# Cross-attention and a quantised feed-forward block on one core: the first block of attention written anew, with work moved from VectorE to GpSimd and ScalarE

## The chip, the core and the metric

The kernel runs on one core of one Trainium2 chip. Its engines are TensorE (PE in the profile; PEld is its weight load), VectorE (DVE), ScalarE (ACT), GpSimd (POOL) and SyncE (SP, which here only starts transfers). Each works through its own queue of instructions in order, and they wait for one another by semaphores. Transfers are started on the queues of SP, POOL and ACT ("SPq", "POOLq", "ACTq" in the profile). The metric is the device time of one execution in microseconds, and the time of a kernel is the median of its runs. The profile comes from one execution, taken by the hardware profiler.

## What is computed

The reference, cut to what matters (`_proj(W, b, x)` is `einsum('oi,bil->bol', W, x) + b[:, None]`):

```python
# x, ctx: (32, 64, 512); 8 heads over the last axis, 64 wide
q = _proj(Wq, bq, layernorm(x)); k = _proj(Wk, bk, ctx); v = _proj(Wv, bv, ctx)
p = softmax(q_h k_h^T / 8)               # per head and batch, 64 x 64
x = x + _proj(Wo, bo, p v_h)
g = silu(layernorm(x) @ dequant(gate))   # 512 -> 1792
u = layernorm(x) @ dequant(up)
x = x + (g * u) @ dequant(down)          # 1792 -> 512
# dequant: (integer - zero) * scale, one zero and one scale
# per 128 input rows and column
```

The projections act on the 64 rows of a batch element, not on the 512 columns. All is float32.

## The kernel before

**Tiling.** Two batch elements of 64 rows fill the 128 partitions: a *pair*. There are 16 pairs, in 4 *blocks* of 4. For each block the kernel does the attention of its pairs, normalises the result, turns it over (`flip`, L557) into a high and a low part (`hTh`, `hTl`, 128x512 for each 128 input columns; `high` L580, `low` L583), and runs the feed-forward on the block: for each of 14 chunks of 128 hidden columns, `gate_up` (L633) does 4 steps of a gate product `pg` and an up product `pu` (four matmuls of 512 columns a step, L642), with a scaling by ScalarE after each of the first three steps (L652, by the quotient of neighbouring scales `s_q`), then SiLU (L655), the product with up (L658), its split into high and low (GpSimd, L668 and L669), and `down` (L674) with its products (L687, L690).

**Weights.** The integers stand in SBUF as float; their zeros are subtracted in place: gate (`ng`) and up (`nu`) by GpSimd (L309), a piece of 256 or 512 columns at a time, down (`nd`) by VectorE (L322). The zeros go to DRAM in 16 and 8 bits (`zeros`, cast by GpSimd, L153) and come back broadcast over the partitions (L289, L295). Weight columns are loaded in groups, the first of 256 columns, the second of 512, by transfers that GpSimd's queue starts (L273, L277).

**The head.** The attention of block 0 cannot lie beside a feed-forward. Its four pairs are done one by one, by a text, `START` (L778), that writes down the order in which steps are issued: "2.apply" is the step `apply` of pair 2. Within the head (`tc.manual_schedule()`, L800) every engine's queue has just this order. The steps of a pair:

- `stats` (VectorE, L396 to L398), `scale` (GpSimd, the power -1/2, L402), `apply` (VectorE, L112): layer norm of the pair's rows into `xn`.
- `k`, `q` (32 small products each, L421), `k_out`, `q_out` (VectorE, bias added on the way out of PSUM, L433); `v` (L456), `v_out` (ScalarE, L466).
- `scores` (L474), `highest` (L486), `less` (L489; both VectorE), `exp` (ScalarE, L502), `sums` (VectorE, L506 and L507), `divide` (GpSimd, L512).
- `turn` (L521; the weights of softmax times Wo), `turn_out` (ScalarE, L531), `weigh` (L538), `residual` (VectorE, two halves of 256 columns, adding the last bias and the rows, L551; then the store of the rows, L554, on SP).
- `stats2`, `scale2`, `apply2`, `flip`, `high`, `low`: the second layer norm and the turning over.

Steps without a pair: `projections` and `biases` lay out the small weights; `zeros`, `broadcast`, `more` (zeros); `gate`, `up`, `more_gate`, `more_up` (loads of weight columns, on GpSimd's queue); `rows` (load of the rows of pairs 4 and 5, on SP); `integers` (one piece L309 each); `scales` (L234, the scales transposed, and `scales_out`, L236); `quotients` (VectorE, L242 to L244, over 128x84); `warm` (idle products on PE, L571). Steps named "behind products" (L821) wait for the last PE work written before them. The head's PSUM tiles are four pairs of banks; they are given back before the first `pg`, so the first gate product (40.07 us in the profile) waits for the last `low`.

**Behind the head** the loop over rounds (L918) issues a step of each of two lanes of `gate_up`, of `down`, of block t+1's attention (`ROUND_STEPS`, L594; there two pairs are done together, "4to" in a tile's name is pairs 4 and 5), and weight pieces (at most so many a round, L910). There a scheduler sets each engine's order. The attention of later blocks has one PSUM tile of two banks (`ps_at`, L885) for all its products in turn: `pk`, `pv`, `pq`, `pss` and so on, each of which waits until the one before has been read. The rows `x` have three buffers (L126), so the rows of pairs 6 and 7 are loaded once those of pairs 0 and 1 have been stored and read for the last time.

## Time and profile before

| | |
|---|---|
| median of 3 runs | 438.89 us (438.71 to 439.97) |
| the profiled execution: its time, its span | 440.32 us, 438.2 us |
| granted TensorE clock, mean of the span | 0.99 |
| busy: PE, PEld, DVE, ACT, POOL | 408.2, 313.8, 329.7, 305.1, 281.7 us |
| last `hTl` of the head ends; first gate product starts | 39.82; 40.07 us |
| POOL's pieces of `nu`, first 256 columns | 30.87 to 34.54 us (start of the last 33.88) |
| POOL issues `ng`, `nu`, `nd` (second group) at | 30.02, 35.72, 36.53 us |
| ACT busy from 10 to 15 us | 0.00 us |
| DVE busy from 10 to 15 us | 4.86 us |

A row of the profile's groups or timeline names the line of the kernel, the engine, the operation, and "out<-in" by the tiles' names with partitions x columns; "x4" is how many instructions are merged in it. In brackets stands how long the engine had been idle and what ended that. The chain of waits follows the work that ended last back to the start, each piece to what released it; "issue" is time in which the engine waited for nothing that the profile shows. The table of stretches gives, for each stretch, each engine's busy time and number of instructions, the clock that TensorE was granted (1.00 is full), the share of the transfer engines and what they moved.

### The profile page before, as it was taken

Reading aid. Unit: us, or ns where it says so; the run is one execution under the profiler, and the core shown is the slowest. Engines: PE = TensorE matmul, PEld = TensorE weight load, DVE = VectorE, ACT = ScalarE, POOL = GpSimd, SP = SyncE. Lnnn points to the kernel's source line nnn. Section 1 sums busy time; section 2 is a strip of 40 time slices with the busy share of each in tenths; the row PEclk is TensorE's granted clock in tenths of the full one; section 3 lists DMA queues with packets and bytes.
Section 4 is the critical chain, followed back from the end, with each engine's and each line's share of the span. In section 5 each row is a group of like instructions: output and inputs, shape, how many; then the busy total and the mean of one; then the engine's idle time right before and its main releaser. Section 6 shows DMA issues by size and latency. Waiting matters only on the chain.

```text
span 438.2 us, 10356 instructions
## 1 busy us (share of the span) xinstructions
PE 408.2 (93%) x4191; PEld 313.8 (72%) x4191; DVE 329.7 (75%) x515; ACT 305.1 (70%) x468; POOL 281.7 (64%) x291
## 2 busy tenths in 40 slices
PE   3777989889999999999999999989999999999993
PEld 3655657557778786887778787767778888887772
DVE  4988476986879885895869885896869655768675
ACT  2243888347787769767888669776788778777771
POOL 4375849676844547575787668775787887774330
PEclk9999989989999999999999999999999999999998
DMA  6299739942021200321010103310000012110002
GB/s 213 60 270 362 246 125 287 331 146 74 1 74 48 72 29 0 96 100 49 1 50 0 52 1 97 96 49 1 1 14 38 1 49 88 57 49 0 2 4 99
DMA packets 20911, 36.54 MB, mean 83 GB/s; under 512 B 1832, under 2 KB 7416, under 8 KB 20856
## 3 DMA queue, kind: packets, MB, share of 16 engines
q1 hardware_dynamic: 14056, 24.20, 16.6%
q0 software_dynamic: 6192, 11.01, 8.7%
q8 instruction: 35, 0.57, 0.5%
q10 hardware_dynamic: 608, 0.59, 0.4%
q14 instruction: 20, 0.16, 0.1%
HBM read 27.37 MB, written 8.42 MB: 82 GB/s over the span
## 4 chain that ended last, share of the span: by engine, by line
PE 75%; DVE 12%; ACT 6%; POOL 3%; issue 2%; DMA 1%; SPq 0%; DVEq 0%; POOLq 0%; ACTq 0%
PE pu L642 21%; PE pg L642 21%; PE pd L687 11%; PE pd L690 10%; DVE y L700 3%; ACT pu L652 1%; ACT pg L652 1%; DVE xn_set L112 1%; DMA x<-in_x_dram 1%; DVE q_e_set L489 1%; PE py L715 1%; POOL ng L309 1%; ACT q_e_set L502 1%; ACT L502 1%; POOL q_e_set L512 1%
## 5 line engine op out<-in xcount | busy, mean ns | idle before, releaser
L700 DVE SCALAR_TENSOR_TENSOR y<-pd,s_all,y 128x512 f32<-128x512 f32 x204 | 150.1, 743 | 42.8 <-PE pd L690 39.7
L652 ACT ACTIVATE pg<-pg,s_q 128x512 f32<-128x512 f32 x168 | 111.7, 666 | 71.0 <-PE pg L642 69.7
L652 ACT ACTIVATE pu<-pu,s_q 128x512 f32<-128x512 f32 x168 | 111.1, 662 | 8.9 <-PE pu L642 7.9
L668 POOL CAST hh<-h 128x512 fp32r<-128x512 f32 x55 | 36.4, 663 | 96.7 <-DVE h L658 93.5
L687 PE MATMUL pd<-hh,nd 128*128 128x512 f32 x224 | 93.0, 415 | 2.8 <-DVE y L700 2.1
L642 PE MATMUL pg<-hTh,ng 128*128 128x512 f32 x224 | 90.9, 406 | 3.8 <-DVE hTl L585 1.6
L642 PE MATMUL pu<-hTh,nu 128*128 128x512 f32 x224 | 91.0, 406 | 1.2 <-POOL nu L309 0.8
L642 PE MATMUL pu<-hTl,nu 128*128 128x512 f32 x224 | 89.5, 399 | 0.0
L642 PE MATMUL pg<-hTl,ng 128*128 128x512 f32 x224 | 89.2, 398 | 0.0
L690 PE MATMUL pd<-hl,nd 128*128 128x512 f32 x224 | 89.1, 398 | 0.0
L669 POOL TENSOR_TENSOR hl<-h,hh 128x512 fp32r<-128x512 f32 x55 | 73.3, 1332 | 4.2
L658 DVE SCALAR_TENSOR_TENSOR h<-pu,s_all,g 128x512 f32<-128x512 f32 x56 | 41.8, 747 | 30.0 <-ACT g L655 20.0
L687 PEld LDWEIGHTS pd<-hh,nd 128*128 128x128 f32 x224 | 42.1, 188 | 19.8 <-DVE y L700 6.3
L339 POOL TENSOR_TENSOR squares<-squares 128x512 f32<-128x512 f32 (+1 forms) x46 | 55.1, 1199 | 1.6
L642 PEld LDWEIGHTS pg<-hTh,ng 128*128 128x128 f32 x224 | 42.4, 189 | 17.5 <-issue 2.7
L642 PEld LDWEIGHTS pu<-hTh,nu 128*128 128x128 f32 x224 | 42.5, 190 | 15.7 <-ACT pu L652 2.2
L642 PEld LDWEIGHTS pg<-hTl,ng 128*128 128x128 f32 x224 | 42.5, 190 | 9.5
L642 PEld LDWEIGHTS pu<-hTl,nu 128*128 128x128 f32 x224 | 42.7, 190 | 9.3
L655 ACT ACTIVATE g<-pg,s_all 128x512 f32<-128x512 f32 x56 | 38.9, 695 | 14.0 <-PE pg L642 12.4
L690 PEld LDWEIGHTS pd<-hl,nd 128*128 128x128 f32 x224 | 42.3, 189 | 8.1 <-DVE hl L666 0.2
L309 POOL TENSOR_TENSOR nu<-nu,z 128x512 fp32r<-128x512 f32 (+1 forms) x16 | 17.4, 1090 | 1.7 <-DMA nu<-in_L_ffn_up_w_dram 1.6
L309 POOL TENSOR_TENSOR ng<-ng,z 128x512 fp32r<-128x512 f32 (+1 forms) x16 | 17.1, 1077 | 0.0
(291 smaller groups left out, 464.8 us busy)
## 6 DMA issues: line engine op xcount, KB each, us to landing
c_set<-in_ctx_dram SPq DMA_DIRECT2D x6, 512.0 KB
x<-in_x_dram SPq DMA_DIRECT2D x6, 512.0 KB
z<-z_dram SPq DMA_DIRECT2D x6, 512.0 KB
ng<-in_L_ffn_gate_w_dram POOLq DMA_DIRECT2D x3, 1024.0 KB, 5.8
nu<-in_L_ffn_up_w_dram POOLq DMA_DIRECT2D x3, 1024.0 KB, 8.9
x_dram<-x SPq DMA_DIRECT2D x6, 512.0 KB
r<-x_dram SPq DMA_DIRECT2D x6, 512.0 KB
out_dram<-r SPq DMA_DIRECT2D x6, 512.0 KB
```

What stands on the lines that cost most here:

```text
L309: nc.gpsimd.tensor_tensor(piece, piece.bitcast(F32), z16[:, m, g, :], ALU.subtract)
L339: nc.gpsimd.tensor_tensor(total[:, :n], total[:, :n], square[:, :n], ALU.add)
L502: nc.scalar.activation(e, e, AF.Exp, scale=SCALE)
L642: nc.tensor.matmul(acc, w[:, g, ts(f, P)], half[:, g, :], start=(g == 0 and half is hi), stop=(g == KT - 1 and half is lo), skip_group_che ...
L652: nc.scalar.activation(acc, acc, AF.Copy, scale=by)
L655: nc.scalar.activation(g_sb, acc, AF.Silu, scale=by)
L658: ins = nc.vector.scalar_tensor_tensor(h_sb, acc, by, g_sb, ALU.mult, ALU.mult)
L668: nc.gpsimd.tensor_copy(hh, h_sb)
L669: ins = nc.gpsimd.tensor_tensor(hl, h_sb, hh.bitcast(F32), ALU.subtract)
L687: nc.tensor.matmul(pd, w, h_hi[t, f], start=(t, f) != LAST, stop=False, skip_group_check=True)
L690: nc.tensor.matmul(pd, w, h_lo[t, f], start=False, stop=True, skip_group_check=True)
L700: ins = nc.vector.scalar_tensor_tensor(y, pd, by, y, ALU.mult, ALU.add)
```

## The change

In block 0 only:

- Pairs 2 and 3: `apply` on GpSimd (`apply_pool`); k leaves PSUM by a ScalarE copy (`k_copy`) and gets its bias from GpSimd in SBUF (`k_bias`). Pairs 0 and 1 stay on VectorE.
- All four pairs: the last bias is added to the rows by ScalarE (`shift`), once `apply` and the statistics have read them; `residual` is then one tensor_tensor over 512 columns.
- `quotients` falls in three: `guards` (GpSimd: zero test and sum), the first two chunks' columns on VectorE at the end of the head (two reciprocals and two products of 128x6), and the other twelve chunks' columns in round 1 behind the head (two and two of 128x36). `s_inv` moves to a pool that lives on.
- `START` is written anew: pairs in the order 0, 2, 3, 1; the loads, integers, warm products and stores move with it.

```diff
-        def quotients():
-
-            s_inv = early.tile([P, 2, NS - FC], F32, tag="s_inv", name="s_inv")
+        s_inv = const.tile([P, 2, NS - FC], F32, tag="s_inv", name="s_inv")
+
+        def guards():
+
             later = s_all[:, 0:2, FC:]
-            nc.vector.scalar_tensor_tensor(s_inv, later, 0.0, later, ALU.is_equal, ALU.add)
-            nc.vector.reciprocal(s_inv, s_inv)
-            nc.vector.tensor_tensor(s_q, s_all[:, 0:2, : NS - FC], s_inv, ALU.mult)
+            nc.gpsimd.tensor_scalar(s_inv, later, 0.0, None, ALU.is_equal)
+            nc.gpsimd.tensor_tensor(s_inv, s_inv, later, ALU.add)
+
+        def quotients(fs: slice):
+
+            for m in range(2):
+                inv, num, quot = (
+                    a.rearrange("p (g f) -> p g f", f=FC)[:, :, fs]
+                    for a in (s_inv[:, m, :], s_all[:, m, : NS - FC], s_q[:, m, :])
+                )
+                nc.vector.reciprocal(inv, inv)
+                newest["DVE"] = nc.vector.tensor_tensor(quot, num, inv, ALU.mult).ins
...
+            def apply_pool(self):
+                nc.gpsimd.tensor_scalar(
+                    self.at["xn"][:, 0, :],
+                    self.x[:, 0, :],
+                    self.mv[:, 0, 0:1],
+                    self.rs,
+                    ALU.subtract,
+                    ALU.mult,
+                )
...
+            def k_copy(self):
+                nc.scalar.copy(self.by_bank("k_eT"), self.pk)
+
+            def k_bias(self):
+                k = self.by_bank("k_eT")
+                b = bqk[:, 1, :].unsqueeze(1).unsqueeze(1).to_broadcast([P, 2, self.n * KT, D])
+                nc.gpsimd.tensor_tensor(k, k, b, ALU.add)
...
             def residual(self):
                 x_heads = self.by_head(self.x)
+                if self.n == 1:
+                    x_h = x_heads.rearrange("p n h d -> p h n d")
+                    nc.vector.tensor_tensor(x_h, self.po, x_h, ALU.add)
+                    return self.keep_rows()
...
+            def shift(self):
+                nc.scalar.activation(self.x, self.x, AF.Identity, bias=bvo[:, 1:2])
...
         START = """
...
+            0.stats 0.scale 0.apply projections 1.stats biases projections_out
+            1.scale 2.stats 0.q biases_out 0.shift 3.stats 2.scale 2.k 2.apply_pool
+            0.k 2.k_copy 0.q_out 1.v 0.k_out 3.scale 2.shift 2.q 1.apply 3.apply_pool
+            1.v_out 0.scores 2.q_out 1.shift 3.k 0.highest 2.k_bias 3.shift 3.q
+            0.less 3.k_copy 1.q zeros 3.q_out 0.exp 2.scores 1.q_out 3.k_bias
+            broadcast 0.v 2.highest 1.k 0.v_out 2.less 2.v 1.k_out 2.exp 3.v 0.sums
+            2.v_out 1.scores gate 3.v_out 3.scores 1.highest 0.divide 3.highest
+            2.sums 0.turn 3.less 2.divide 0.turn_out 1.less 3.exp 0.weigh 2.turn
+            1.exp 3.sums up rows 2.turn_out 1.sums 3.divide 2.weigh 0.residual
+            1.divide 3.turn 2.residual 3.turn_out integers 2.stats2 1.turn more
+            integers scales 1.turn_out 0.stats2 3.weigh integers scales_out 1.weigh
+            integers 3.residual 3.warm 3.warm more_gate 3.stats2 0.scale2 1.residual
+            3.scale2 0.apply2 more_up 1.stats2 0.flip 1.warm 0.high 3.apply2 2.scale2
+            0.low 3.flip 1.scale2 2.apply2 3.high integers 1.apply2 2.flip integers
+            3.low 1.flip 2.high integers 1.high 2.low guards 1.low integers quotients
+            1.warm
...
                 elif step == "quotients":
-                    quotients()
+                    quotients(slice(0, FIRST // P))
+                elif step == "guards":
+                    guards()
...
+                if r == 1:
+                    with tc.issue_after(newest["DVE"]):
+                        quotients(slice(FIRST // P, FC))
```

Behind the head the order of the instructions on PE, ACT and POOL is unchanged. On DVE the second part of the quotients stands among the statistics of pairs 4 and 5, and the second `apply` of that set stands ahead of its `k_out` where it stood behind it.

## The prediction

> **What bounds the kernel now.** I read the page's busy shares first: PE 93% of the span, so after the head (everything before the first gate product) PE is the bound, and a change in the head can give at most what it brings that product forward, and only if block 1's first steps follow. So I read the chain of waits from 35 to 47 us (start, length, what):
>
> ```profile
> 37.06 0.69 DVE s_inv L243
> ...
> 37.77 0.24 DVE s_q L244
> 38.02 1.80 DVE hTl L585 x3
> 39.82 0.25 issue
> 40.07 0.70 PE pg L642 x2
> ...
> 44.48 0.64 PE pu L642 x2
> 45.11 1.02 PE pv_4to L456 x16
> ```
>
> The head ends on DVE: the last hTl at 39.82 lets PE start at 40.07, and the quotients stand ahead of three of the four hTl. From 40.07 the chain is PE, with pv of pairs 4 and 5 in it. Next, busy time by stretch (us; then PE, PEld, DVE, ACT, POOL, granted clock, DMA share, GB/s):
>
> ```profile
> 10.00:15.00 5.00, 4.97 (x212) 4.36 (x204) 4.86 (x13) 0.00 (x0) 1.67 (x4) 1.00 0.07 16
> 15.00:20.00 5.00, 3.13 (x140) 2.54 (x136) 4.90 (x10) 2.52 (x4) 1.06 (x2) 1.00 0.41 111
> 30.00:35.00 5.00, 2.90 (x13) 2.15 (x14) 4.70 (x12) 0.59 (x1) 4.54 (x9) 1.00 0.79 195
> ```
>
> DVE is full (4.7 to 4.9 of 5 us) while ACT and POOL have room until 20 us: the place the change draws from. Last, DVE's timeline after the head:
>
> ```profile
> 39.73 1.27 DVE L396 BATCH_NORM_STATS2 st_4to<-x 128x6 f32<-128x512 f32 x2
> 41.26 0.17 DVE L398 TENSOR_SCALAR rs_4to<-mv_4to 128x2 f32<-128x2 f32 x1
> 42.33 1.38 DVE L112 TENSOR_SCALAR xn_set<-x,mv_4to,rs_4to 128x512 f32<-128x512 f32 x1 [0.90 <-POOL rs_4to L402]
> 43.63 1.21 DVE L433 TENSOR_TENSOR k_eT_set<-pk_4to,bias 128x1024 f32<-128x1024 f32 x1
> 44.76 0.53 DVE L112 TENSOR_SCALAR xn_set<-x,mv_4to,rs_4to 128x512 f32<-128x512 f32 x1
> ```
>
> pv (L456) uses the PSUM tile that k's bias add (L433) reads, and there is one: pv starts at 45.04, 0.20 after that add ends (44.84). PE's weight loads waited 0.36 for it. So DVE's chain from hTl to L433 is already a second bound, just behind PE.
>
> **The head, part by part.** Taken off DVE: two normalisations (L112, 0.55 each: 1.1), two k biases (0.69 long, 0.62 apart: 1.25), the residual of four pairs from 0.82 (two halves) to about 0.62 (one tensor_tensor as L433: 4 x 0.2 = 0.8), and the quotients (0.24 + 0.68 + 0.24, about 1.1) from ahead of the last hTl. Together 4.2 us.
>
> Not all of it comes out. I set each engine's new written order out with these durations, each step starting at the later of its engine's free time and its last operand (0.05 us on, 0.16 from DVE to POOL). The same walk over the old order ends the last hTl at 40.2, against the 39.82 of the trace, so 0.35 is its error. Over the new order it gives 37.3, and 37.6 if DVE's normalisations lose time beside POOL. About 1.5 us turns into new DVE waits: 0.7 for pair 0's k, now third on PE in the stretch where 32 products took 1.1 us; 0.6 for pair 3's exp, behind pair 0's copy on ACT; the rest for pair 3's weigh and single latencies. Last hTl at **37.2, 2.6 earlier**; with an error of 0.7 either way.
>
> What I cost at nothing, and its cover. POOL's two normalisations are not in the trace: one input and two scalars, between the cast L668 (0.61) and the two-input L309 (1.17 with 512 columns). I take 0.85, and the walk's end doesn't move up to 1.8, since pair 2's q would wait only past 12.8 and xn is there at 10.9. POOL's k biases (1.04, as the division L512 x4): pair 2's is done at 13.7, read at 15.9; pair 3's at 16.6, read at 19.6. ACT's additions, four shifts (0.65, as the exp L502 or L466) and two k copies (0.57 as L531), 3.7 us, lie mostly in ACT's empty stretch; the last ends at 15.5, and pair 0's exp is wanted at 15.7, so past 0.2 us more each tenth delays that exp. POOL's queue: the zero casts go from 12.1 to 13.7, so the broadcast lands near 23, wanted at 27.4; the last nu piece ends at 37.8 instead of 34.5, read past 40; guards take some 0.6 between the pieces. The 512-column gate load stays at 30.0; up and down loads are issued at 31.9 and 32.7 instead of 35.7 and 36.5. On SP, the load of pairs 6 and 7 waits for the store of pair 1, now last; its rows are wanted near 62: 20 us of cover.
>
> Here a rule speaks against the change. The rows: two-input POOL work of 128x512 takes 1.04 to 1.17, the same size on DVE 0.69. The Trainium skill, "GPSIMD Engine Reference", opening and § 3.1, calls this engine the wrong choice for elementwise arithmetic, two inputs at half DVE's speed. By the rule alone the moved work loses; by the rows it has slack, and the sum stays.
>
> **Behind the head, where most of it is given back.** The new order of instructions on DVE has four small operations after the last hTl (first quotients), then the statistics of pairs 4 and 5 with two reciprocals of 36 columns among them, then *both* normalisations ahead of k's bias; before, one. A reciprocal took 0.20 for 8 columns (L507) and 0.68 for 84 (L243), so 0.38 for 36, some 0.34 apart, and 0.19 with a product of 0.18 for 6.
>
> 1. Last hTl 37.2; first quotients 2 x (0.19 + 0.18), 0.65 with overlap; statistics start 37.8.
> 2. To the end of rs_4to 1.70 (39.73 to 41.43) plus 0.68 for the reciprocals: 40.2.
> 3. POOL's power, 0.15 later and 0.72 long: 41.05. The two remaining products hide there.
> 4. Two normalisations. Alone 1.07 (2 x 0.535); beside POOL's subtractions:
>
> ```profile
> 86.53 2.27 DVE L112 TENSOR_SCALAR xn_set<-x,mv_4to,rs_4to 128x512 f32<-128x512 f32 x2
> ```
>
> Before, only the first (1.38) met one, since POOL then waited 1.65 for nu until 45.07. With nu loaded earlier, the second will meet one too. I take 2.05: 43.1.
> 5. k's bias 1.21: 44.3, pv at **44.5**, against 45.04.
>
> Behind pv every engine's order is as before, and PE (to 52) and ACT (to 60) carry the chain, so what is left at pv stays to the end. As a sum: 2.6 from the head, less 0.67 (the statistics started 0.09 ahead of the last hTl's end, now 0.6 behind), less 0.68 (reciprocals), less 0.75 (2.05 of normalisations where 1.30 stood, 42.33 to 43.63) = **0.5 us**. The profiled execution took 440.32 (span 438.2), the median of the runs is 438.89; I take the difference from each: 439.8 for such an execution, **438.4** for the median.
>
> Bounds: last hTl 0.7 each way; normalisations 1.07 to 2.98 (twice the slowest, 1.49 at 87.3), so -1.0 to +0.9; reciprocals of 36 between the 0.20 and 0.68 rows each, -0.3 to +0.6. All together -2.5 to +1.7.
>
> **Rivals.** (1) *The gain stays.* If the normalisations run near 0.54 each (POOL still waiting for nu or its zeros) and the last hTl is at 36.7 or earlier, pv starts near 43: 1.5 to 2.6 faster, 436.8. For: PE had only 0.36 of slack to lose. Against: the 2.27 row. (2) *The clock drops.* PE's queue ahead of pv now ends near 42.1, so PE stands 2.4 us idle; before, at most 1.5 there. The rows (us, PE busy, granted clock, DMA share, GB/s):
>
> ```profile
> 57.00:60.00 3.00, 1.62 (x6) 1.00 0.93 316
> 61.00:63.50 2.50, 2.50 (x8) 0.50 0.06 22
> 64.00:65.00 1.00, 1.00 (x6) 1.00 0.35 113
> 88.00:91.00 3.00, 1.34 (x6) 1.00 0.34 111
> 91.50:94.50 3.00, 3.00 (x8) 0.50 0.26 92
> ```
>
> After 3 us in which PE was busy 1.3 to 1.6 the clock was half for 3.4 us (60.5 to 64, 91.25 to 94.7). If 42 to 44.5 does the same, 3.4 us at half speed while PE is the bound cost up to 1.7: 0.5 faster becomes 1.2 slower, and with normalisations of 2.5 it is **440.4, slower**. It decides where PE's idle fills over half of such a window. Against: 38.5 to 40.0 stood idle at full clock. The Trainium skill, "TensorE: Matmul & The Clock Gate", Part 1, says that the window runs free of the kernel's start and is 3.4 us; the two stretches here, 30.7 apart and 3.4 long, agree, and by the rule executions would differ in this. (3) *The head doesn't shorten as read*: exp, weigh or POOL late, last hTl 38.2 or later. Past 37.7 pv is later than before: +0.5 to +1.2, 439.6.
>
> **How the numbers follow.** Forecast 0.50, rival 1 0.27, rival 2 0.16, rival 3 0.07. 0.3% is 1.3 us, about what a measurement of this kernel tells from no change. Forecast and rival 3 lie within it; rival 1 is faster; of rival 2 nearly all is slower. Faster 0.27, same 0.58, slower 0.15. The range, 436.6 to 440.3, leaves out the fastest end of rival 1 and the slow end of rival 2.
>
> **What would show it.** In the new profile: last hTl near 37.2; four tiny DVE operations behind it; two L112 rows of pairs 4 and 5 together near 2 us ahead of k's bias; PE idle about 2.4 us with "DVE k_eT_set" as releaser ahead of pv; pv near 44.5; nu's first 512 columns without a wait. Wrong if pv starts before 43.5 or after 45.5, or if half clock appears between 43 and 50.

## The result and the profile after

The kernel after takes **445.38 us** (443.15 to 446.16, four runs) against 438.8 in the runs of the kernel before beside them: ratio 1.0136, 95% interval 1.0109 to 1.0162. The ratios here and below are of the executions in the fast state, which leaves out one of f_full (446.60), and they are not those of the two medians. The kernel after is 6.6 us slower where 0.5 faster was forecast, far outside the range. Its profiled execution took 444.75 (span 442.9, clock 0.974), 4.4 above that of before; the pair of profiles shows two thirds of the loss, and the rest is in executions that were not profiled.

Line numbers below are those of each kernel's own file; in the kernel after L541 is the division, L550 the turn, L567 weigh, L580 the residual, L319 a weight piece, L412 a power, L453 k's and q's bias, L485 v, L611 idle products, L625 hTl.

The steps on VectorE behind the head came as written. Its timeline after the last hTl (start, length, engine, line, operation):

```profile
41.70 0.68 DVE L625 TENSOR_TENSOR hTl<-ph,hTh 128x512 fp32r<-128x512 f32 x1
42.30 0.18 DVE L253 RECIPROCAL s_inv<-s_inv 128x6 f32<-128x6 f32 x1
...
42.89 1.28 DVE L406 BATCH_NORM_STATS2 st_4to<-x 128x6 f32<-128x512 f32 x2
...
44.73 0.11 DVE L408 TENSOR_SCALAR rs_4to<-mv_4to 128x2 f32<-128x2 f32 x1
...
45.67 2.68 DVE L112 TENSOR_SCALAR xn_set<-x,mv_4to,rs_4to 128x512 f32<-128x512 f32 x2 [0.63 <-POOL rs_4to L412]
48.27 1.21 DVE L453 TENSOR_TENSOR k_eT_set<-pk_4to,bias 128x1024 f32<-128x1024 f32 x1
```

The four small operations, both normalisations ahead of k's bias, and pv at 49.54: 7.16 behind the last hTl, where 7.3 was forecast. But that hTl ends at **42.38**, not 37.2. pv is 4.5 later than before (45.04) and the span 4.7 longer. Of the 4.5, 2.6 stand ahead of the last hTl (39.82 before) and 1.9 behind it (7.16 where it was 5.22); the 1.9 were in the forecast. So the whole miss of the forecast, 5.2 us, is made ahead of the last hTl.

The chain of waits (start, length, what) goes through the head like this:

```profile
26.43 0.10 POOL nu L283
...
27.27 1.06 POOL q_e_set L541
28.33 0.04 issue
28.38 2.13 PE pe L550 x64
...
31.00 1.10 PE po L567 x32
...
36.29 1.19 POOL rs L412 x2
37.48 1.89 POOL nu L319 x3
39.37 0.86 POOL s_inv L243
...
41.28 3.60 issue
...
49.54 1.09 PE pv_4to L485 x16
```

Before, its end was VectorE; now GpSimd stands in it with a load's issue ("nu L283" is the step 'up'), a division, powers, pieces of nu and the guards. Its last part is to be read with care: behind GpSimd's last piece stand 3.60 us of "issue", and the timeline has GpSimd waiting there for VectorE's statistics (3.64, for rs_4to). So from 37 us on it is VectorE, with two normalisations beside these pieces, that holds the head. And the 64 products of two turns take 2.13 where before two turns of 32 took 0.69 each. The table of stretches says why (us; PE, PEld, DVE, ACT, POOL, granted clock, DMA share, GB/s):

```profile
10.00:15.00 5.00, 5.00 (x216) 4.64 (x212) 3.53 (x9) 3.52 (x7) 4.90 (x4) 1.00 0.03 8
20.00:24.00 4.00, 1.42 (x64) 1.01 (x57) 3.10 (x6) 1.11 (x4) 2.98 (x3) 0.99 1.07 291
24.00:30.00 6.00, 4.51 (x139) 4.08 (x142) 3.97 (x10) 1.50 (x4) 3.55 (x5) 0.50 0.58 158
30.00:35.00 5.00, 4.97 (x94) 4.28 (x87) 3.59 (x10) 1.00 (x3) 3.99 (x7) 0.58 1.06 308
```

The work was moved as intended: VectorE 3.53 of 5 us from 10 to 15 instead of 4.86, ScalarE 3.52 instead of nothing. Then TensorE is busy 1.42 of 4 us from 20 to 24, where before it was busy 2.77:

```profile
20.00:24.00 4.00, 2.77 (x120) 2.00 (x116) 3.93 (x8) 1.79 (x3) 2.02 (x3) 1.00 0.68 168
```

And from about 24 to 34.3 it has half clock (0.50), which the head before never had. Here is TensorE at that place:

```profile
18.02 0.21 PE L441 MATMUL pk<-w_T,c_set 64*64 64x64 f32 x1 [0.65 <-issue]
...
22.15 0.69 PE L550 MATMUL pe<-w_T,q_e_set 64*64 64x64 f32 x32 [1.88 <-POOL q_e_set L541]
23.55 0.45 PE L567 MATMUL po<-v_set,k_eT_set 64*64 64x64 f32 x13 [0.70 <-ACT k_eT_set L560]
24.38 0.79 PE L567 MATMUL po<-v_set,k_eT_set 64*64 64x64 f32 x18 [0.38 <-issue]
...
28.38 2.13 PE L550 MATMUL pe<-w_T,q_e_set 64*64 64x64 f32 x64 [0.39 <-POOL q_e_set L541]
```

Three waits: 1.88 for pair 0's division, 0.70 for ScalarE's copy, and inside pair 0's weigh a stop of 0.38 after 13 of 32 products for nothing that the profile shows ("issue"). An earlier stop of this kind, 0.65, stands ahead of the last product of pair 1's k. The kernel before has none in its head.

### The profile page after: what moved, and what is told of

It reads as the page before. It is cut to its first block, busy times and chain, and to the rows that moved or that the text cites. A ratio compares the mean times of both kernels' runs of the same rounds, so it can differ in the third digit from the quotient of the medians.

```text
span 442.9 us, 10372 instructions
## 1 busy us (share of the span) xinstructions
PE 412.3 (93%) x4191; PEld 318.1 (72%) x4191; DVE 329.6 (74%) x512; ACT 308.9 (70%) x474; POOL 289.6 (65%) x297
## 4 chain that ended last, share of the span: by engine, by line
PE 74%; DVE 7%; POOL 6%; ACT 6%; issue 4%; DMA 1%; SPq 0%; POOLq 0%; DVEq 0%; ACTq 0%
PE pu L682 21%; PE pg L682 20%; PE pd L727 11%; PE pd L730 10%; DVE y L740 2%; ACT pu L692 1%; PE py L755 1%; ACT pg L692 1%; POOL q_e_set L541 1%; DVE xn_set L112 1%; DMA x<-in_x_dram 1%; POOL nu L319 1%; POOL rs L412 1%; POOL xn_set L426 1%; ACT q_e_set L531 1%
## 5 line engine op out<-in xcount | busy, mean ns | idle before, releaser
L698 DVE SCALAR_TENSOR_TENSOR h<-pu,s_all,g 128x512 f32<-128x512 f32 x56 | 41.8, 747 | 29.6 <-ACT g L695 19.9
L319 POOL TENSOR_TENSOR nu<-nu,z 128x512 fp32r<-128x512 f32 (+1 forms) x16 | 17.3, 1090 | 0.0
L319 POOL TENSOR_TENSOR ng<-ng,z 128x512 fp32r<-128x512 f32 (+1 forms) x16 | 16.8, 1058 | 0.0
```

The lines of the kernel that those rows point to most:

```text
L319: nc.gpsimd.tensor_tensor(piece, piece.bitcast(F32), z16[:, m, g, :], ALU.subtract)
L698: ins = nc.vector.scalar_tensor_tensor(h_sb, acc, by, g_sb, ALU.mult, ALU.mult)
```

## The experiments

Theory A: the new written order brings separate losses into the head (half clock after TensorE's idle; 'up' ahead of the last divisions on GpSimd; normalisations beside GpSimd's pieces), which add up. Rivals: B, moved work costs more where it goes than it saves; C, one chain stands behind all. In the table below, hTl is the end of the last hTl of the profiled execution and pv the start of the products of v of pairs 4 and 5. Both are of one execution of each kernel, and these are not equally early: GpSimd's first normalisation, ahead of all that the edits of the kernel after move, starts between 8.95 (d_gate) and 10.17 us (a_nu_late). So a difference in hTl of about 1 us between two rows does not tell much by itself; what lies within one profile, as from hTl to pv, is firmer. The diffs of `START` show only the part of a line that changes, and leave out mends that were shown before.

| kernel | median us | ratio to before, interval | hTl | pv |
|---|---|---|---|---|
| before | 438.89 | | 39.82 | 45.04 |
| after | 445.38 | 1.0136, 1.0109 to 1.0162 | 42.38 | 49.54 |
| a_warm | 443.31 | 1.0106, 1.0070 to 1.0141 | 42.98 | 50.13 |
| a_up_late | 444.02 | 1.0129, 1.0103 to 1.0155 | 41.31 | 48.46 |
| a_nu_late | 443.35 | 1.0108, 1.0084 to 1.0132 | 40.73 | 47.42 |
| a_rest_late | 444.68 | 1.0119, 1.0072 to 1.0166 | 42.86 | 49.78 |
| b_shift | 438.76 | 0.9989, 0.9967 to 1.0011 | 38.87 | 44.09 |
| b_pool | 440.16 | 1.0017, 0.9998 to 1.0036 | 41.59 | 46.83 |
| b_quot | 441.83 | 1.0057, 1.0039 to 1.0075 | 38.06 | 41.93 |
| c_three | 445.43 | 1.0124, 1.0093 to 1.0156 | 42.23 | 49.76 |
| c_four | 444.91 | 1.0115, 1.0071 to 1.0159 | 44.23 | 51.53 |
| d_gate | 444.98 | 1.0140, 1.0116 to 1.0165 | 42.44 | 49.59 |
| d_dve | 443.54 | 1.0090, 1.0061 to 1.0119 | 42.56 | 49.74 |
| d_mend | 442.65 | 1.0085, 1.0052 to 1.0119 | 41.32 | 47.94 |
| e_quiet | 443.59 | 1.0102, 1.0067 to 1.0138 | 42.34 | 49.58 |
| e_full | 443.08 | 1.0091, 1.0063 to 1.0119 | 42.10 | 49.81 |
| f_full | 442.50 | 1.0083, 1.0045 to 1.0122 | 39.49 | 46.26 |
| f_best | 443.53 | 1.0121, 1.0059 to 1.0182 | 42.90 | 48.35 |
| g_pow | 441.44 | 1.0054, 1.0027 to 1.0081 | 43.08 | 47.75 |
| g_load | 438.69 | 0.9998, 0.9982 to 1.0014 | 39.45 | 44.68 |

### Single mends of the kernel after

**a_warm**: idle products where TensorE stood.

```diff
-2.v_out 1.scores gate 3.v_out 3.scores 1.highest
+2.v_out 1.scores gate 3.v_out 3.scores 3.warm 3.warm 3.warm 1.highest
...
-2.sums 0.turn 3.less
+2.sums 0.turn 3.warm 3.less
```

> The changed kernel with three more idle products written behind pair 3's scores and one behind pair 0's turn, nothing else; they fill the stretch from 20.3 to 23.5 us in which PE stood idle ahead of the half clock of 24.0 to 34.3. Clock theory (that idle halves the clock, and slow turn and weigh products carry the head's loss): full clock from 24 to 34, pair 3's residual at 30 instead of 32.2, last hTl at 40.2 instead of 42.4, kernel 2 us faster, near 443.3. Port theory (the head's loss lies in the normalisations beside POOL at 37 to 40): the clock may be full, but DVE only waits elsewhere, last hTl within 0.7 of 42.4, kernel unchanged within 0.7. If the added products delay pair 0's turn: up to 0.5 slower.

Full clock from 24 to 34, each turn and weigh 0.69 again; from pair 0's turn to pair 3's residual 8.9 us instead of 10.04, although an idle step and a stop of 0.85 lie in between, so the clock is worth at least 1.1 there. But the 12 idle products ran 2.86 us and put the turn off by 1.0; the last hTl is no earlier. And the "issue" stop is still there, now among idle products:

```profile
23.15 0.69 PE L550 MATMUL pe<-w_T,q_e_set 64*64 64x64 f32 x32
23.77 0.48 PE L611 MATMUL idle<-x,ident 128*128 128x256 f32 x1
25.11 0.81 PE L611 MATMUL idle<-x,ident 128*128 128x256 f32 x3 [0.85 <-issue]
```

**a_up_late**: the load 'up' behind the last division.

```diff
-1.exp 3.sums up rows 2.turn_out 1.sums 3.divide 2.weigh 0.residual 1.divide 3.turn
+1.exp 3.sums rows 2.turn_out 1.sums 3.divide 2.weigh 0.residual 1.divide up 3.turn
```

> The changed kernel with the first load of nu written behind pair 1's division, so that the divisions of pairs 3 and 1 no longer queue on POOL behind a load that waits for pair 2's turn on PE. Queue theory (this load costs the head pair 3's division, ready at 25.0, started at 27.3): division of pair 3 at 25.2, its turn at 26.4 to 27, last hTl 1.2 to 2 us earlier, kernel 1 to 2 us faster. Clock theory alone: PE stays at half clock until 34.3, products of 1.1 us carry the chain, gain below 0.7. Against both: nu lands 2.5 us later and its first piece on POOL (37.5 now) waits, which costs nothing up to about 5 us.

Pair 3's turn 27.84 instead of 28.38, last hTl 1.07 and pv 1.08 earlier. Half clock also ended earlier, at 30.4 instead of 34.2, so this gain need not be that of the queue alone.

**a_nu_late**: one piece of nu ahead of pair 3's power, the others and the guards behind the turning products.

```diff
-more_gate 3.stats2 0.scale2 1.residual 3.scale2
+more_gate 3.stats2 0.scale2 1.residual integers 3.scale2
...
-3.high integers 1.apply2 2.flip integers 3.low 1.flip 2.high integers 1.high 2.low guards 1.low integers quotients
+3.high 1.apply2 2.flip 3.low 1.flip behind_guards 2.high 1.high 2.low integers 1.low integers quotients integers
```

> The changed kernel with the first piece of nu ahead of pair 3's power on POOL, and guards and the last three pieces behind pair 1's flip on PE, so that the last two normalisations of the head run beside idle POOL. Port theory: those two take 1.1 instead of 2.88 us, last hTl at 40.6 instead of 42.4, kernel 1.8 us faster (443.6), unless the pieces are then late for the first products. Clock theory: the normalisations were long for another reason and stay over 2 us, kernel within 0.5.

The last two normalisations of the head, in a_nu_late, with no piece and no guards on GpSimd beside them (only a power of 128x1, until 38.03):

```profile
37.46 1.15 DVE L112 TENSOR_SCALAR xn_set<-x,mv,rs 128x512 f32<-128x512 f32 x2
```

In the kernel after, beside pieces and guards:

```profile
37.23 2.88 DVE L112 TENSOR_SCALAR xn_set<-x,mv,rs 128x512 f32<-128x512 f32 x2
```

Last hTl 1.65, pv 2.12 earlier, and the clock was half here too, from 23 to 33, so the gain is not the clock's. The Trainium skill, "SBUF — State Buffer", section "Who interferes with whom", says that VectorE's tensor_scalar, in its two-port modes, and GpSimd contend for one shared port pair, and that the one that has it blocks the other for a whole instruction. These rows agree.

**a_rest_late**: the second part of the quotients in round 3.

```diff
-                if r == 1:
+                if r == 3:
                     with tc.issue_after(newest["DVE"]):
                         quotients(slice(FIRST // P, FC))
```

> The changed kernel with the second part of the quotients in round 3 instead of 1; the scheduler then puts its two reciprocals behind h of chunk 0 and they leave the chain from statistics to k's bias. By the prediction's sum for the stretch behind the head: 0.7 us less from last hTl to pv (7.16 in the changed kernel, so 6.5), kernel 0.7 us faster, unless the clock's half speed falls elsewhere. Rival (PE, not DVE, sets pv's start once the head ends late): pv no earlier, kernel unchanged within 0.3.

From last hTl to pv 6.92 instead of 7.16: 0.24, not 0.7. The two reciprocals of 36 columns were never worth 0.68.

### One part of the change on the kernel before

**b_shift**: last bias on ScalarE and the residual in one piece, old order.

```diff
+                if self.n == 1:
+                    x_h = x_heads.rearrange("p n h d -> p h n d")
+                    nc.vector.tensor_tensor(x_h, self.po, x_h, ALU.add)
+                    return self.keep_rows()
...
-projections_out 1.apply 2.stats 0.k biases_out 2.scale
+projections_out 1.apply 2.stats 0.k biases_out 0.shift 1.shift 2.scale
...
```

> The kernel before, in its old written order, with one part of the change: the four additions of the last bias on ScalarE (pairs 0 and 1 early, pair 3's behind its normalisation, pair 2's behind the copy of its v) and the residual as one addition of 512 columns. Theory A (the change loses through the new arrangement of the head: half clock, 'up' ahead of a division on GpSimd, normalisations beside GpSimd; its parts in themselves do no harm): VectorE loses 4 x 0.2 us, so the last hTl ends at 39.0 to 39.6 instead of 39.82 and the products of v of pairs 4 and 5 start at 44.3 to 44.9 instead of 45.04; time 438.0 to 438.9. Theory B (each part that is moved costs more where it goes than it saves): pair 3's addition stands ahead of pair 0's exponential on ScalarE, last hTl at 40.0 or later, time 439.3 or more. No half clock before 45 us by A.

Last hTl 0.95 earlier and pv as much; this part does what the forecast charged for it (0.8). Its profile has half clock too, from 31.4 to 34.8, and the head is no longer for it. The median moves by less than can be told (-0.1%, interval -0.3 to +0.1).

**b_pool**: pairs 2 and 3 normalised and their k biased by GpSimd, old order.

```diff
-2.k 3.apply 1.scores broadcast 0.highest 2.apply 2.k_out
+2.k 3.apply_pool 1.scores broadcast 0.highest 2.apply_pool 2.k_copy 2.k_bias
...
-1.divide 3.k_out
+1.divide 3.k_copy 3.k_bias
```

> The kernel before, in its old written order, with one part of the change: pairs 2 and 3 normalised by GpSimd (2.08 us each by the profile of the kernel after), their k copied out by ScalarE (0.57) and biased by GpSimd (1.28). VectorE loses 2.35 us of work, but in the old order pair 3's k comes late: its bias then lands 1.0 to 1.8 us later than before (copy 0.57, wait for a division on GpSimd, 1.28) and stands ahead of the loads and divisions on GpSimd. Theory A (the parts do no harm in themselves): last hTl within 0.6 of 39.82, time 438.3 to 439.5. Theory B (moved work costs more where it goes): pair 3's scores and all behind them 1 us or more late, last hTl 40.6 or later, time 440 or more.

Last hTl 1.77, pv 1.79 later, as theory B has it for this part. But TensorE again stops for "issue", 0.94 until 24.09, and has half clock from 33.1 to 40. When VectorE has its quotients it is only 0.2 late (`s_q` at 37.99; before 37.77); then it waits 1.10 for ScalarE's `hTh`, whose turning products run at half clock. So what the moved work costs by itself is not shown. The median is 0.2% up, not to be told from no change.

**b_quot**: guards on GpSimd and quotients in two parts, old order.

```diff
-more_up 2.apply2 0.flip 1.low 2.flip 3.apply2 0.high quotients 3.flip
+more_up guards 2.apply2 0.flip 1.low 2.flip 3.apply2 0.high 3.flip
...
-3.high 2.low 3.low
+3.high 2.low 3.low quotients
```

> The kernel before, in its old written order, with the quotients' part of the change: guards on GpSimd behind its second loads, the first two chunks' columns behind the last low, the rest in round 1. VectorE is relieved of 1.1 us ahead of the last three hTl: last hTl at 38.7 instead of 39.82. In this kernel the order on VectorE behind the head comes out otherwise than in the kernel after: k's bias of pairs 4 and 5 stands ahead of the first quotients, so the products of v start near 42.7, and ScalarE's first scalings, which need the quotients, near 43 instead of 40.8. By the view that the products of v carry the gain: 2 earlier, time 437 to 438. By the view that TensorE's two lanes then stand still for the scalings: the gain is lost in the wait, time 438.5 to 440.

Head 1.76 shorter, pv at 41.93, and still slower: k's bias came ahead of the first quotients, so ScalarE's first scaling, which needs them, starts at 42.29 after 4.95 us idle (before: at 40.81). pv early is worth nothing when something else is the bound.

### Mends together, and the stop

**c_three** (two idle steps, 'up' late, pieces late) and **c_four** (and the second quotients in round 3):

```diff
-gate 3.v_out 3.scores 1.highest
+gate 3.v_out 3.scores 3.warm 3.warm 1.highest
```

> The kernel after with three mends at once: two idle product steps of pair 3 behind its scores (8 products, about 1.9 us by the 2.86 that 12 took), the load 'up' behind the last division, and three pieces of nu and the guards behind the turning products. Theory A (three separate losses): they add up. Last hTl 42.38 less 1.1 (load), less 1.65 (pieces), less about 1 (clock) = 38.0 to 39.2, the products of v start 7.2 less 0.85 (normalisations of pairs 4 and 5 alone again) later, 44.3 to 45.6; time 438.5 to 441. Full clock from 24 to 34. Theory C (one chain behind all three, so that mending one mends the others): last hTl 40.2 or later, no better than the best single mend by over 0.6, time 442 to 443.5.

> As the kernel with three mends, and the second part of the quotients in round 3 of the loop instead of round 1, so that its two reciprocals (0.34 us apart) no longer stand in the statistics of pairs 4 and 5. By the single run of that edit, which brought the products of v 0.24 us forward behind the last hTl: 0.2 to 0.7 us earlier at the products of v than with three mends, time 0.2 to 0.7 less than it, 438 to 440.5 by theory A, 441.5 to 443 by theory C.

Theory A failed: the mends do not add up. Two reasons show. 'up' late lets nu land late, and the piece of nu that I had put ahead of pair 3's power held GpSimd's queue 2.48 and 3.37 us. And the stop grew. In c_three:

```profile
22.02 0.69 PE L550 MATMUL pe<-w_T,q_e_set 64*64 64x64 f32 x32
23.42 0.33 PE L567 MATMUL po<-v_set,k_eT_set 64*64 64x64 f32 x5 [0.70 <-ACT k_eT_set L560]
24.83 0.62 PE L567 MATMUL po<-v_set,k_eT_set 64*64 64x64 f32 x26 [1.08 <-issue]
```

It comes after 5 products of the weigh, not 13, with 8 idle products put ahead; with 12 (a_warm) it comes after the first idle product behind the turn. In all three 126 products, each with its weight load, lie between it and the stop before it. So TensorE stops at a fixed place in its own list of instructions.

**d_gate**: the first gate load behind pair 2's division on GpSimd.

```diff
-1.scores gate 3.v_out 3.scores 1.highest 0.divide 3.highest 2.sums 0.turn 3.less 2.divide 0.turn_out
+1.scores 3.v_out 3.scores 1.highest 0.divide 3.highest 2.sums 0.turn 3.less 2.divide gate 0.turn_out
```

> The kernel after with the step 'gate' (the first gate load, 0.89 us on GpSimd's queue, ahead of pair 0's division there) moved behind pair 2's division. Theory D (GpSimd's queue order and the loads hold up TensorE at 20 to 25 us): pair 0's division starts at 20.0 instead of 21.04, its turn on TensorE at 21.1 instead of 22.15; the load then lands after 26, so the idle that the profile calls 'issue' inside pair 0's weigh (0.38 us at 24.0, up to 1.36 in other runs, always while the transfer engines are full) is gone or below 0.2; last hTl 0.8 to 2 us earlier than 42.38, products of v as much earlier than 49.54; time 442 to 443.5. Theory E (the clock alone decides: TensorE idle for some 2 us in a stretch of 3.4): idle ahead of the turn falls from 1.88 to about 0.8, half clock does not begin by 24, turns and weighs take 0.7 to 1.2 for one or two, last hTl 1.5 to 3 earlier. Theory F (neither matters, another chain carries the head): last hTl within 0.5 of 42.38.

The turn starts 1.8 us earlier (0.9 of it stand already at the first stop, which ends at 17.07 instead of 18.02), and the stop takes all of it:

```profile
20.36 0.69 PE L550 MATMUL pe<-w_T,q_e_set 64*64 64x64 f32 x32 [0.79 <-POOL q_e_set L541]
21.76 0.45 PE L567 MATMUL po<-v_set,k_eT_set 64*64 64x64 f32 x13 [0.70 <-ACT k_eT_set L560]
24.49 0.80 PE L567 MATMUL po<-v_set,k_eT_set 64*64 64x64 f32 x18 [2.29 <-issue]
```

In none of the kernels above that have the new order does TensorE pass this place before 24.4. So D and E fail, and F's number came with a reason of its own: the stop.

**d_dve**: GpSimd's part undone in the new order.

```diff
-2.apply_pool
+2.apply
...
-2.k_copy
+2.k_out
```

> The kernel after with GpSimd's part undone: pairs 2 and 3 normalised and their k biased by VectorE, in the same written order. VectorE gets 2.35 us of work back, GpSimd loses 6.7 (two of 2.08, two of 1.28). If the new written order is what loses (with the same waits at 20 to 40 us), last hTl is at 42 or later, up to 44, time 445 to 447. If GpSimd's slower work is what loses (a normalisation there took 2.08 us where the forecast had 0.85), last hTl is earlier than 42.38 by over 0.5, time 443.5 or less.

Last hTl 42.56 against 42.38, though VectorE has 2.35 us more to do: what was taken off VectorE ahead of this place bought nothing. The time, 443.54, is not longer either, so the last hTl is as the first branch of the expectation has it and the time as the second.

**d_mend**: five mends (gate, 'up', guards early, all pieces late, second quotients in round 3).

```diff
-more_gate 3.stats2 0.scale2 1.residual
+more_gate 3.stats2 0.scale2 guards 1.residual
...
-3.low 1.flip 2.high integers 1.high 2.low guards 1.low integers quotients
+3.low 1.flip behind_integers 2.high integers 1.high 2.low integers 1.low integers quotients
```

> The kernel after with five mends in its written order: 'gate' behind pair 2's division, 'up' behind the last division, the guards in GpSimd's idle time ahead of pair 3's second power, all four pieces of nu behind the turning products (none ahead of a power, which is where the kernel with three mends waited 2.48 us for the load of nu), and the second part of the quotients in round 3. Theory A (separate losses add up): last hTl 42.38 less 1 (gate), less 1.1 (up), less 1.65 (pieces) = 38.6, by the clock 37.8 to 39.6; the products of v 6.3 to 6.9 behind it, 44.5 to 46; time 438.4 to 440.5. Theory C (one chain behind all of them): last hTl 40.5 or later, time 442 or more.

Last hTl 41.32: the stop is 2.01 (until 24.97), and half clock follows it from 25 to 36.

What ends the stop? The profile lists one packet of 0.02 MB at a time on a queue of its own, "q8 instruction". In the whole kernel after there are 35:

```profile
q8 instruction: 35, 0.57, 0.5%
```

When the packet starts (the quarter of a microsecond in which it does), and TensorE:

| kernel | packet starts | stop | TensorE goes on |
|---|---|---|---|
| after | 21.25 | 0.38 | 24.38 |
| a_up_late | 22.00 | 0.51 | 24.45 |
| a_warm | 22.00 | 0.85 | 25.11 |
| a_rest_late | 22.25 | 0.72 | 24.85 |
| c_three | 22.00 | 1.08 | 24.83 |
| c_four | 23.00 | 1.36 | 25.71 |
| b_pool | 21.50 | 0.94 | 24.09 |
| d_gate | 22.00 | 2.29 | 24.49 |
| d_mend | 22.50 | 2.01 | 24.97 |

TensorE goes on 2.4 to 3.1 us after the packet starts. In a_nu_late and d_dve, with packets at 21.75, it comes to this place at 24.76 by other waits and does not stop. c_four and d_mend stop once more, 126 and 127 products on (0.88 and 0.27, until 29.7), and b_quot, in the old order, stops 0.66 until 27.66, after a packet at 25.25. The Trainium skill, "Runtime: NRT & Kernel Launch", section "Instruction fetch mechanics", says that an engine's instructions come in blocks of 256 over a queue of its own; 126 products with their loads are 252, which is close, and the 4191 products and as many loads of the kernel would, by this page's figure, fill an estimated 33 such blocks where 35 packets are listed. It calls the crossing of a block mostly hidden; here it cost up to 2.3 us. Theory I: the packet is late because zeros, context and gate weights are being moved from 18 to 24.

**e_quiet**: gate late, and the zeros' broadcast and the context of pairs 4 and 5 moved from 17.9 and 18.9 to 24.5 and 26.4.

```diff
-broadcast 0.v 2.highest
+0.v 2.highest
...
-1.exp 3.sums up rows 2.turn_out
+1.exp 3.sums up broadcast rows context 2.turn_out
```

> The kernel after with the first gate load behind pair 2's division, and with the first broadcast of zeros and the load of the context of pairs 4 and 5 (512 KB) moved on SP's queue from 17.9 and 18.9 us to the place of the load of rows, some 26 us. So the transfer engines have nothing to move from 17 to 22.4 us. Theory I (TensorE stops inside pair 0's weigh because its next 256 instructions are loaded late, behind these transfers; it cannot pass that point before 24.4 us whatever comes earlier): the packet on the instruction queue starts by 19.5 instead of 21.4 to 22.6, the 'issue' idle in pair 0's weigh (2.29 in the kernel with the gate load moved) is under 0.3, pair 0's weigh ends by 22.6, pair 2's turn starts at 22.7 to 23.2 and not at 24.97. TensorE's idle in 20 to 24 us then shrinks and half clock starts later or not at all; last hTl 40 to 41.5, time 441.5 to 443.5. Theory J (the stop has nothing to do with the transfers): the stop ends at 24.4 to 25 as in the others, time 444.5 to 445.5.

The packet starts at 20.5 (Theory I had it by 19.5, but this profile is about 1 us behind d_gate's from the start), and the stop in the weigh is gone; the first one, in pair 1's k, is 0.62:

```profile
21.53 0.69 PE L550 MATMUL pe<-w_T,q_e_set 64*64 64x64 f32 x32 [0.79 <-POOL q_e_set L541]
22.93 0.83 PE L567 MATMUL po<-v_set,k_eT_set 64*64 64x64 f32 x32 [0.70 <-ACT k_eT_set L560]
23.71 0.69 PE L550 MATMUL pe<-w_T,q_e_set 64*64 64x64 f32 x32
```

Against d_gate, from which it differs by the two transfers alone, pair 0's turn starts 1.17 later and pair 3's residual 2.85 earlier (d_gate, then e_quiet):

```profile
32.24 0.69 DVE L580 TENSOR_TENSOR x<-po,x 128x512 f32<-128x512 f32 x1 [1.17 <-PE po L567]
...
29.39 0.69 DVE L580 TENSOR_TENSOR x<-po,x 128x512 f32<-128x512 f32 x1 [0.56 <-PE po L567]
```

Clock full until 40, pair 3's residual at 29.39 (32.19 in the kernel after), pair 1's at 31.14. The gain is then given back on GpSimd: pieces of ng wait 2.45 for the late zeros ahead of the first power, and the last pair of normalisations takes 3.06 beside nu.

**e_full**: the same with d_mend's other mends.

```diff
-1.exp 3.sums rows 2.turn_out
+1.exp 3.sums broadcast rows context 2.turn_out
```

> The kernel with five mends, and the broadcast and the context load late as well, so that all losses named so far are mended together. Theory I and A (instruction load, clock, 'up', pieces beside normalisations are the whole loss): the stop of 2.01 us in pair 0's weigh goes, last hTl 37.4 to 39.4 (the forecast's walk: 37.2), the products of v 6.3 to 6.9 behind it at 44 to 46, time 437.5 to 440.5. Rival (something else holds the head beyond these): last hTl 40 or later, time 442 or more.

No stop in the weigh; residuals at 29.42 and 31.16; zeros 2.70 late, half clock from 25 to 29 and from 35.5 to 43; last hTl 42.10. The rival of the expectation holds.

**f_full**: zeros cast between GpSimd's normalisations and broadcast early, context still late.

```diff
-1.v 0.k_out 3.scale
+1.v 0.k_out zeros 3.scale
...
-1.shift 3.k 0.highest
+1.shift 3.k broadcast 0.highest
```

> All the mends as before, but the casts and the first broadcast of zeros go early (casts between GpSimd's two normalisations, broadcast near 14.5) instead of late: in the two kernels with the late broadcast the pieces of ng waited 2.45 and 2.70 us for the zeros on GpSimd's queue, ahead of the first power of the second layer norm. The context load stays late. By the theory that instruction load, clock, GpSimd's queue and normalisations beside GpSimd are the whole loss of the head: no stop in pair 0's weigh, the third and fourth residual by 29.4 and 31.2, the first normalisation of the second layer norm by 32.2 (34.2 with the late broadcast), last hTl 37.5 to 39.5, the products of v 6.5 to 7.7 behind, 44.5 to 46.5, time 438 to 441. Rival: hTl 40.5 or later by yet another wait, time 442.5 or more.

In this profile there is no stop in the weigh (0.62 in pair 1's k) and no half clock at all; from 20 to 24 the transfer engines have next to nothing:

```profile
20.00:24.00 4.00, 2.51 (x132) 2.14 (x128) 3.76 (x9) 2.04 (x4) 2.42 (x3) 1.00 0.02 4
24.00:30.00 6.00, 4.41 (x193) 3.70 (x186) 5.69 (x14) 2.23 (x5) 4.99 (x7) 1.00 0.84 225
```

Last hTl 39.49, pv 46.26, span 438.1 as before's 438.2. But the profiled execution is the shortest of seven: five others lie between 441.5 and 444.7 and one at 446.6, median 442.5.

**f_best**: as f_full, quotients whole inside the head.

```diff
-                    quotients(slice(0, FIRST // P))
+                    quotients(slice(0, FC))
...
-0.low 3.flip
+0.low quotients 3.flip
```

> As the kernel with all mends and early zeros, but the quotients in one part (two reciprocals and two products of 128x42) inside the head, behind the first hTl, where VectorE waited 1.2 us for GpSimd; nothing of them is left behind the head. By the forecast's price list for the part behind the head (0.67 for the first quotients, 0.68 for the reciprocals): last hTl as there or up to 0.5 later, and the products of v 5.2 to 6.3 behind it instead of 6.5 to 7.7; time 437.5 to 440, up to 1 less than the kernel with two parts. If the split behind the head cost nothing, the two are equal to within 0.4.

From last hTl to pv 5.45 instead of 6.77: in f_full the first quotients cost 1.3 behind the head, twice the price list's 0.67, since their two products of six columns took 0.55 and 0.50 beside GpSimd's pieces of nu (0.17 in the kernel after, with GpSimd idle). But this execution stopped for 1.89 at the block before (until 19.63), has half clock twice in the head and a late gate load (3.01 on GpSimd). No version of the kernel after beats the kernel before.

**g_pow**: f_full with round 1 again for the second quotients, and the second loads behind the last powers.

```diff
-3.scale2 0.apply2 more_up 1.stats2
+3.scale2 0.apply2 1.stats2
...
-1.scale2 2.apply2
+1.scale2 more_up 2.apply2
```

> The kernel with all mends and early zeros, and the two second loads (nu 0.95 us and nd 0.83 us to issue) moved on GpSimd's queue behind the last two powers of the second layer norm; there they stood ahead of them, and VectorE waited 1.16 us. If this is the last of the loss in the head: powers of pairs 2 and 1 at 34 instead of 35.6, last two normalisations at 34.6 to 35.4 instead of 36.2, last hTl 37.6 to 38.6 (the forecast's walk: 37.2; the kernel with all mends 39.49), the products of v 44.2 to 45.4, time 437.5 to 441. An execution in which the instruction load comes late is 1 to 3 us longer. If it is not, last hTl 39 or later.

The profiled execution stopped 1.45 until 19.59 (packet at 17.25) and ng waited 3.07 for the gate load, so it does not answer its question. The median, 441.44, is the lowest of all versions of the kernel after.

**g_load**, the reverse test: the kernel before with its first gate load at 15.2 instead of 19.9.

```diff
-2.k_out 0.less 0.v 1.highest
+2.k_out 0.less 0.v gate 1.highest
...
-0.divide 3.k gate
+0.divide 3.k
```

> The reverse test on the kernel before: its first gate load (512 KB) stands behind pair 0's v on GpSimd's queue, near 15.2 us where GpSimd is idle, instead of 19.9. It takes nothing from GpSimd (pair 1's division even has 0.85 less ahead of it), but the transfer engines are full from about 16 to 21 us, when TensorE's instructions for 21.5 us on are loaded (packet at 19.3 in the kernel before, no stop). Theory I (a late instruction load stops TensorE): the packet starts at 20.3 or later, TensorE stops 0.5 to 2.5 us at about 21.5 with 'issue', residuals and last hTl 0.5 to 2 later than 25.5 and 39.82, time 439.5 to 441. Theory J (loads and instruction load have nothing to do with one another): no stop, last hTl 39.2 to 39.9, time 438.2 to 439.

The transfer engines are full, and the packet is not late (19.0; before 19.25), no stop, last hTl 39.45:

```profile
16.00:18.00 2.00, 1.39 (x71) 1.15 (x64) 1.97 (x4) 1.58 (x3) 0.00 (x0) 1.00 0.86 223
18.00:20.00 2.00, 1.45 (x72) 1.11 (x64) 1.93 (x6) 0.95 (x2) 1.08 (x2) 1.00 1.03 269
```

So Theory I holds only in part: moving the transfers away takes the stop away, but a gate load alone does not make one. In d_gate, too, the packet is late (22.0) although the gate load is issued only at 22.43. The zeros alone do make one. In f_best and g_pow nothing but their broadcast was moving around the packet ahead of the first stop, and TensorE, in f_full, f_best and g_pow, shows:

```profile
18.49 0.21 PE L441 MATMUL pk<-w_T,c_set 64*64 64x64 f32 x1 [0.62 <-issue]
...
19.63 0.21 PE L441 MATMUL pk<-w_T,c_set 64*64 64x64 f32 x1 [1.89 <-issue]
...
19.59 0.21 PE L441 MATMUL pk<-w_T,c_set 64*64 64x64 f32 x1 [1.45 <-issue]
```

In f_full the packet started at 16.0, ahead of the broadcast (from 16.25), in the other two at 17.0 and 17.25, inside it (from 15.0 and 16.0). The next packet came with nothing else moving in all three, as in e_quiet and e_full: about 2 us after TensorE had gone on from the first stop. In the kernels of the table of packets that have this first stop it came 3.2 to 5 us after it. Whether the context adds to what the zeros do, and why the packet waits, is open.

## Why the prediction was wrong

**Failed: "Last hTl at 37.2, 2.6 earlier".** It ended at 42.38, 2.6 later. The walk "set each engine's new written order out with these durations": TensorE's instructions were taken as always there, its products as always at full clock, and GpSimd beside VectorE's normalisations cost it 0.3. Where the prediction states a time of its walk it stands in the first column (us):

| | prediction | after | e_quiet | f_full |
|---|---|---|---|---|
| pair 0's turn starts | | 22.15 | 21.53 | 21.52 |
| pair 2's turn starts | | 24.97 | 23.71 | 23.71 |
| pair 3's turn starts | | 28.38 | 26.62 | 25.87 |
| pair 3's residual starts | | 32.19 | 29.39 | 28.75 |
| GpSimd issues gate's second load | 30.0 | 31.76 | 32.51 | 30.82 |
| GpSimd issues up's second load | 31.9 | 34.67 | 34.40 | 33.81 |
| last two normalisations start | | 37.23 | 36.77 | 36.20 |
| how long they take | | 2.88 | 3.06 | 1.16 |
| last hTl ends | 37.2 | 42.38 | 42.34 | 39.49 |

What the runs showed in its place:

- *TensorE's instructions and its clock.* From pair 0's turn to pair 3's residual the kernel after takes 10.04 us, and e_quiet, without the stop in the weigh and at full clock, 7.86. So the two together are worth 2.2 there; the clock is at least 1.1 of it (a_warm). They cannot be told apart further, since the stop is part of the idle ahead of the half clock. At the last hTl their worth is seen between d_mend, which has both, and f_full, which has neither and otherwise the same mends, but for the zeros and the context, whose move takes the stop away: 41.32 and 39.49.
- *GpSimd beside the last two normalisations*: 2.88 against 1.15, so 1.7, where the prediction gave 0.3 ("37.6 if DVE's normalisations lose time beside POOL") though it showed the 2.27 row from behind the head. a_nu_late gets 1.65 of it back at the last hTl.
- *'up'*, which stands ahead of the last divisions on GpSimd and waits for pair 2's turn: 1.07 in a_up_late, part of which may be the clock's.

These do not add up, as theory A had it, and with all of them mended f_full's last hTl is still 2.3 later than forecast. Its rows show where, though no run tested it:

```profile
28.31 2.55 POOL L319 TENSOR_TENSOR ng<-ng,z 128x256 fp32r<-128x256 f32 x4 [0.72 <-DMA ng<-in_L_ffn_gate_w_dram]
32.19 0.70 POOL L243 TENSOR_SCALAR s_inv<-s_all 128x84 f32<-128x84 f32 x1
32.97 0.35 POOL L244 TENSOR_TENSOR s_inv<-s_inv,s_all 128x84 f32<-128x84 f32 x1
...
36.20 1.16 DVE L112 TENSOR_SCALAR xn_set<-x,mv,rs 128x512 f32<-128x512 f32 x2 [1.16 <-POOL rs L412]
```

The pieces of ng wait for the gate load, which f_full has late; the guards, 1.05 where the prediction had "some 0.6", stand ahead of the second power; and VectorE waits for the last two powers.

**"The same walk over the old order ends the last hTl at 40.2, against the 39.82 of the trace, so 0.35 is its error"**: a test on an order that is paced by VectorE, which hides what TensorE cannot do. Before, TensorE's packet starts at 19.25 and no stop follows, so nothing in that comparison could fail on it.

**GpSimd's normalisation at 0.85** took 2.08. The bound in "the walk's end doesn't move up to 1.8" was passed, and no run shows a loss from it: without GpSimd's part (d_dve) the head is no shorter. The k bias was 1.28 against 1.04, the shift 0.72 against 0.65.

**Behind the head the forecast held**: first quotients 0.51 (0.65), to the end of rs_4to 1.95 (2.38), power 0.83 (0.85), normalisations 2.68 (2.05), k's bias 1.21 (1.21); 7.16 together (7.3). That the sum is so close is in part luck: it was too low on the normalisations by 0.6, and too high on the stretch to rs_4to by 0.4, where the reciprocals stand (0.34 each, but a_rest_late shows 0.24 for both). PE's idle with k_eT_set as releaser was 0.99 and not 2.4; the first products ran at half clock, which lasted from 41.0 to 44.4.

**The rivals.** Rival 3 ("the head doesn't shorten as read: exp, weigh or POOL late") names the right place, weigh and GpSimd, at a chance of 0.07 and a price of 0.5 to 1.2 where pv was 4.5 late. Rival 2 has the right mechanism at the wrong place: half clock was looked for between 43 and 50, behind the head, and came in it, from 24 to 34, where idle was being added too. (It came once more, until 44.4, so this sign of being wrong was there, as was pv after 45.5.) Its condition, idle "over half of such a window", is not what its two rows show: TensorE was idle 1.38 and 1.66 of 3 us there, and no run measured where the limit lies.

**Open.** Why the instruction packet waits; how much of the loss the clock makes alone; the 2.3 us that f_full's last hTl is still late; and why its executions differ by 4.8 us (439.9 to 444.7) and more when that of its profile is as short as before's. The first stop (0.62, 1.89 and 1.45 us in f_full, f_best and g_pow), which is long when the zeros are ahead of the packet, would explain it, but only one execution of each was seen. So in the medians less than half of the loss comes back in f_full (442.50 from 445.38, against 438.8 before) and some 60% in g_pow (441.44); the rest no run accounts for.

## What to carry to other kernels

Before work is moved to make an engine ahead of TensorE faster, look whether TensorE can go faster there: a stop marked "issue" in the middle of one group of products, at the same number of products in each version, is a floor that work done earlier does not move. Look then at the instruction packets and at what is being transferred ahead of them. A transfer counts twice, by its time in the queue that issues it and by what it collides with, instruction packets included. And a walk over queues that fits the old order has been tested only on what bound the old order.

## What was not expected of the hardware

- In the head of these kernels the instruction packets start 3.3 us or more apart; TensorE went on 2.3 to 3.1 us after a packet's start, and stood up to 2.3 us when it was late. A broadcast of zeros by itself made it late (1.89 and 1.45 us), a load of weights did not.
- GpSimd's normalisation of 128x512 with two scalars took 2.08 us, longer than its two-input addition of the same size (1.28); VectorE's takes 0.54.
- The place of the stop is counted in instructions and its end in time: idle products put ahead move it to an earlier step, and while zeros and context were moving ahead of it in the new order, it still ended between 24.4 and 25.7.
- Four idle steps, 12 of their 16 products ahead of the turn in 2.86 us, kept the clock full from 24 to 34 and cost what they gave.
